# A graph layer and a mixture of experts in one kernel: scatters, bias adds, tile loads and block rows are put in another order

## Chip, cores and metric

The kernel runs on one NeuronCore of a Trainium2 chip. The metric is the device time in microseconds (us), and the time of a kernel is the median of its runs.

## What is computed

The input is a matrix x of 6250 nodes with 256 features, and a list of 206,250 edges that is sorted by destination. First comes an attention layer over the graph, then a mixture of 16 experts of which each node uses two. Cut to what matters:

```
xn  = layernorm(x);  hh = (xn @ W) as 8 heads of 32
e   = exp(leaky_relu(s_src[src] + s_dst[dst]))          # per edge and head
out = segment_sum(hh[src] * e / segment_sum(e), dst)     # per node
x   = x + elu(layernorm(out + xn) * gamma + beta)

y   = layernorm(x)
top-2 experts of y @ gate_w + gate_b, their softmax weights g
moe = sum over the two of g * (relu(y @ w1[e] + b1[e]) @ w2[e] + b2[e])
x   = x + layernorm(y + moe) * gamma2 + beta2
```

## The kernel before

**The edge loop.** The edges are cut into tiles of 128 and 31 tiles make a chunk (`CT`), so there are 52 chunks. A chunk is worked on in four groups of 8, 8, 8 and 7 tiles (`GROUPS`). For each tile, GpSimd (POOL) issues one indirect DMA that gathers 128 rows of the table, with 280 floats each, into a buffer `hx` (L199). A group has one `hx`, and there are four of them. VectorE builds two sets of one-hot matrices (`oh` L977, `ohT` L984), TensorE fetches the destination's part with them (`pm` L992), VectorE makes the edge weights and multiplies the gathered rows in place (L1008), and TensorE sums the rows into the accumulator `agg` (L1011). A group's `hx` is free again after its last `agg` matmul. At the end of a chunk the accumulator goes to `carry` (L1025) and is stored in `accd`. The destination values of a chunk (`abw`, `dlr`) are loaded two chunks ahead by `fetch`, at the start of a chunk, on the queue of SyncE (SP).

**Node blocks.** The nodes form 49 blocks of 128. Once all edges of a block are in, `node_block` loads its sums (`a`, L570) and rows (`xb`, L574) on SP, normalises, leaves y in `acc[:, b, :]` (L602) and finds the top two experts. It is called at the end of the chunk that completes the block.

**Parts and rounds.** The blocks are divided into rounds, and the rounds into parts (`ROUNDS`). When the last block of a part is done, `part_due` calls `routing`, which gives every pair of node and expert a row (`pos`), and puts three sorts of work into queues: `scat`, two scatters for each block, which write y to a buffer in DRAM by expert (`scatter`, L800, an indirect DMA of POOL); `bias`, one step for each block, which adds the two experts' second bias to `acc` (`biases`, L815 to L820); and `due`, the expert tiles that are full. A round's last part flushes all tiles that are left. There are 143 tiles in all.

**A tile** passes through four steps, one group apart: `weights` loads its rows (`xr`, L834) and w1; `turned` loads w2 and transposes the rows (L851); `hidden` multiplies by w1 (L860) and applies the ReLU (L869); `rows_out` multiplies by w2 (L875), copies to `yr` (L877) and stores it in `yg`. All its loads are on SP.

**`some`** is called after each group and takes from the queues: up to four scatters; one bias step if no scatter is waiting; then the next step of each tile under way; then one new tile, if its part has no scatter waiting. A bias add changes the rows that the scatters of its block read, so it must wait for them. The sum `pb` lies in PSUM in a tile `pt`, of which there is one for all transposes and small products.

**After the loop** the queues are emptied, and `result` gathers each node's two expert rows (`got`, L899), adds them, normalises and stores the block.

The order in which the instructions finally stand on each engine is set by a scheduler of the language, which keeps to the dependencies and may let an instruction pass others that are not ready.

Of the kernel before, what the change touches and what calls it, by code (L numbers as in the profile page):

```python
# [10 lines left out]
F32 = mybir.dt.float32  # L11
# [9 lines left out]
P = 128  # L21
# [4 lines left out]
LARGE = 40.0  # L26
CT = 31
GROUPS = (8, 8, 8, 7)
SLACK = 24


ROUNDS = ((10, 14, 18, 22, 26, 30, 34, 36), (43,), (49,))


@with_exitstack
def kernel(
# [20 lines left out]
    nc = tc.nc  # L57
    nc.scalar.preload_act_table_set("natural_log_exp_and_others")
    N, C = x.shape
# [8 lines left out]
    NK = -(-NE // CE)  # L68
# [11 lines left out]
    parts = []  # L80
# [101 lines left out]
    acc = const.tile([P, NB, C], F32, name="acc")  # L182
# [28 lines left out]
    with tc.tile_pool(name="a1", bufs=1) as a1, tc.tile_pool(name="a3", bufs=3) as a3, tc.tile_pool(  # L211
        name="aps", bufs=4, space=bass.MemoryType.PSUM
# [92 lines left out]
        for n in GROUPS:  # L305
# [11 lines left out]
        pb = aps.tile([P, 2 * H], F32, name="ph")  # L317
        nc.tensor.matmul(
            pb, lhsT=ex.to_broadcast([2 * H, P]), rhs=ident[: 2 * H, : 2 * H], start=True, stop=True
# [41 lines left out]
        when = {}  # L361
# [184 lines left out]
    with tc.tile_pool(name="w2", bufs=2) as w2_, tc.tile_pool(name="w3", bufs=3) as w3_, tc.tile_pool(  # L546
        name="rt", bufs=1
# [10 lines left out]
        def clear(r):  # L558

            for t in range(0, PAGES[r], ZR):  # L560
                n = min(ZR, PAGES[r] - t)
                nc.sync.dma_start(
                    xg[r][t * P : (t + n) * P, :].rearrange("(p j) c -> p j c", p=P),
                    zero[:, None, :].to_broadcast([P, n, C]),
                )
# [231 lines left out]
        def scatter(i, b, k):  # L797
            r = parts[i][2]
            n = P if b < NB - 1 else LAST
            t = nc.gpsimd.indirect_dma_start(  # L800
                out=xg[r][:, :],
                out_offset=bass.IndirectOffsetOnAxis(ap=pos[k][:n, b : b + 1], axis=0),
                in_=acc[:n, b, :],
                in_offset=None,
            )
            for _, o in scattered[r]:
                tc.declare_no_dep(t.ins, o.ins, reason="each pair has a row of its own")
            for o in read[r]:
                tc.declare_no_dep(t.ins, o.ins, reason="a tile that was due takes no more pairs")
            scattered[r].append((i, t))  # L810

        def biases(i, b):

            pt = wk.tile([E, P], F32, name="pt")
            nc.tensor.transpose(pt, shares[i][:, b - parts[i][0], :], ident)  # L815
            gt = e2.tile([E, P], F32, name="gt")
            nc.scalar.copy(gt, pt)
            pb = wk.tile([P, C], F32, name="pt")
            nc.tensor.matmul(pb, lhsT=gt, rhs=b2r, start=True, stop=True)
            nc.vector.tensor_add(acc[:, b, :], acc[:, b, :], pb)  # L820

        taken = []
        stored = []
# [92 lines left out]


        scat, due, bias = deque(), deque(), deque()
        at = [None, None, None]

        def some():
            for _ in range(min(4, len(scat))):
                scatter(*scat.popleft())
            if bias and not scat:
                biases(*bias.popleft())
            if at[2]:
                rows_out(*at[2])
            at[2] = hidden(*at[1]) if at[1] else None
            at[1] = turned(*at[0]) if at[0] else None
            at[0] = None  # L930
            if due and not any(t[0] == due[0][0] for t in scat):
                t = due.popleft()
                at[0] = weights(*t)

        def part_due(i):
            lo, hi, _, _, mt = parts[i]
            assert not any(t[0] < i - 1 for t in bias)
            routing(i)
            scat.extend((i, b, k) for b in range(lo, hi) for k in range(2))
            bias.extend((i, b) for b in range(lo, hi))  # L940
            due.extend((i, j) for j in range(mt))
# [4 lines left out]
        def fetch(k):  # L946

            after = fetched[-2][2:] if k > 1 else ()
            r0 = load(base_i[:, k : k + 1], 0, N - 1, engines=(ET.SP,), after=after)
            abw = w3_.tile([P, S3], BF16, name="abw", bufs=4)  # L950
            nc.sync.dma_start(abw, abd[ds(r0, P), :])
            dlr = w3_.tile([P, CT, P], U8, name="dlr")
            t0 = k * CT
            came = nc.sync.dma_start(
                dlr.rearrange("p t e -> p (t e)"),
                dlb[t0 : t0 + CT, :].rearrange("t e -> (t e)").partition_broadcast(P),
            )
            fetched.append((abw, dlr, came))

        weighed = []  # L960
        carry = None
        fetch(0)
        fetch(1)
        for k in range(NK):
            after = used[-2] if k > 1 else ()
            if k + 2 < NK:
                fetch(k + 2)
            abw, dlr, _ = fetched[k]
            t0 = k * CT
            agg = wps.tile([P, RA], F32, name="agg")  # L970
            g0 = 0
            for n in GROUPS:
                with ExitStack() as order:
                    if len(weighed) > 1:
                        order.enter_context(tc.issue_after(weighed[-2].ins))
                    oh = w3_.tile([P, n, P], F32, name="oh")
                    nc.vector.tensor_tensor(  # L977
                        oh,
                        along[:, None, :P].to_broadcast([P, n, P]),
                        dl[:, t0 + g0 : t0 + g0 + n, None].to_broadcast([P, n, P]),  # L980
                        ALU.is_equal,
                    )
                    ohT = w3_.tile([P, n, P], BF16, name="ohT")
                    nc.vector.tensor_tensor(  # L984
                        ohT,
                        dlr[:, g0 : g0 + n, :],
                        along[:, None, P:].to_broadcast([P, n, P]),
                        ALU.is_equal,
                    )
                pm = wps.tile([P, n * (S3 + H)], F32, name="pm")  # L990
                for g in range(n):
                    nc.tensor.matmul(  # L992
                        pm[:, g * S3 : (g + 1) * S3], lhsT=ohT[:, g, :], rhs=abw, start=True, stop=True
                    )
                hx, gathered = early.pop(0) if k == 0 else gather(k, g0, n)
                uv = w3_.tile([P, n, 2 * H], F32, name="uv")
                with ExitStack() as order:
                    if weighed:
                        order.enter_context(tc.issue_after(weighed[-1].ins))
                    nc.vector.tensor_reduce(  # L1000
                        uv, pm[:, : n * S3].rearrange("p (n t h) -> p n h t", n=n, t=3), AX.X, ALU.add
                    )
                nc.vector.tensor_tensor(uv, uv, hx[:, :, RA:], ALU.mult)  # L1003
                wt = pm[:, n * S3 :].rearrange("p (n h) -> p n h", n=n)
                nc.vector.tensor_tensor(wt, uv[:, :, :H], uv[:, :, H:], ALU.max)
                rows = hx[:, :, :RA].rearrange("p n (h d) -> p n h d", h=H)
                weighed.append(
                    nc.vector.tensor_tensor(rows, rows, wt.unsqueeze(3).to_broadcast([P, n, H, D1]), ALU.mult)  # L1008
                )
                for g in range(n):  # L1010
                    nc.tensor.matmul(  # L1011
                        agg,
                        lhsT=oh[:, g, :],
                        rhs=hx[:, g, :RA],
                        start=(g0 == 0 and g == 0),
                        stop=(carry is None and g0 + g == CT - 1),
                    )
                g0 += n
                some()
            if carry is not None:  # L1020
                shift = w2_.tile([P, P], F32, name="shift")
                nc.vector.tensor_scalar(shift, imp, down[:, k - 1 : k], None, op0=ALU.is_equal)
                nc.tensor.matmul(agg, lhsT=shift, rhs=carry, start=False, stop=True)
            carry = w2_.tile([P, RA], F32, name="carry")
            nc.scalar.copy(carry, agg)  # L1025
            r1 = load(base_w[:, k : k + 1], 0, DUMP, engines=(ET.Activation,), after=after)
            sent = nc.scalar.dma_start(accd[ds(r1, P), :], carry)
            used.append((sent,))
            for b in when.get(k, ()):
                node_block(b)  # L1030
                for i, p in enumerate(parts):
                    if b == p[1] - 1:
                        part_due(i)
            if k < len(ROUNDS):
                clear(k)
        while scat or due or bias or any(at):
            some()
        for i, p in enumerate(parts):
# [35 lines left out]
```

## Time and profile before

| | |
|---|---|
| median of 3 runs | 3372.06 us (3367.0 to 3377.96) |
| profiled execution | 2816.95 us, its span 2814.9 us |
| granted TensorE clock, mean | 0.817 |
| last gather of the loop / last tile stored | 2458 us / 2783 us after the span's start |
| busiest engines | TensorE 1842.8 us, POOL 1765.1 us, VectorE 1606.7 us |
| moved by DMA | 549 MB, 195 GB/s |

The profile shows one execution, and that execution was shorter than the timed runs. Durations below are from it. In the lines of the profile PE is TensorE, DVE is VectorE, ACT is ScalarE, POOL is GpSimd and SP is SyncE. A group's line gives its line in the code, the engine, the operation, what it writes and reads and how often, then its busy time and the mean in ns, then the engine's idle time ahead of it and what ended most of that. A line of waits gives the total in us, how often, and the longest. A line of the timeline gives the start, the duration, and in brackets the idle time before it and what ended it; "issue" means that nothing which the profile shows was waited for.

### The profile page before, as it was taken

What the parts mean: (1) busy time and instruction counts of PE and PEld (TensorE: products, weight loads), DVE (VectorE), ACT (ScalarE), POOL (GpSimd) and SP (SyncE); (2) the same over time, 40 slices, a digit from 0 to 9 for tenths busy, and PEclk for the clock granted to TensorE, in tenths of its full rate; (3) what the DMA queues carried; (4) which work ended last, traced back from release to release, by engine and by line L of the source; (5) the groups of instructions that cost most, each with busy time, mean ns of one, the idle gap of its engine ahead of it and who ended that gap; (6) DMA issues with size and microseconds to landing.
All of it is one profiled execution on the core that took longest, in us unless ns stands there. A gap on an engine that the chain in (4) does not pass through costs nothing. (4 is left out here: it accounts for less than half of the span.)

```text
span 2814.9 us, 33324 instructions
## 1 busy us (share of the span) xinstructions
PE 1842.8 (65%) x9507; PEld 1480.1 (53%) x9507; DVE 1606.7 (57%) x3479; ACT 447.1 (16%) x1606; POOL 1765.1 (63%) x1866
## 2 busy tenths in 40 slices
PE   7456666656656737638648638646888877866674
PEld 5334444435535526527536427535677666754564
DVE  7646666664763754845737645736456746645521
ACT  4100000001001102002011002010222212222332
POOL 3577777777774774766747765757476776617501
PEclk9777777867877968969869769868898989977898
DMA  7795554546547547547556547556788877848986
GB/s 211 206 318 149 139 143 133 144 137 214 141 135 208 168 133 237 148 142 225 143 167 211 140 139 228 143 163 191 236 266 260 261 229 241 265 137 289 298 277 188
DMA packets 374371, 549.11 MB, mean 195 GB/s; under 512 B 97974, under 2 KB 271500, under 8 KB 374180
## 3 DMA queue, kind: packets, MB, share of 16 engines
q0 software_dynamic: 89904, 263.85, 32.8%
q1 hardware_dynamic: 232408, 237.42, 27.4%
q10 hardware_dynamic: 51868, 45.63, 4.8%
q8 instruction: 78, 1.28, 0.2%
q14 instruction: 113, 0.93, 0.1%
HBM read 468.55 MB, written 78.15 MB: 194 GB/s over the span
## 5 line engine op out<-in xcount | busy, mean ns | idle before, releaser
L199 POOL DMA_INDIRECT hx<-table,src_sb x1612 | 1543.8, 958 | 714.4 <-issue 416.1
L1011 PE MATMUL agg<-hx,oh 128*128 128x264 f32 x3224 | 994.3, 469 | 336.0 <-DVE hx L1008 335.6
L1011 PEld LDWEIGHTS agg<-hx,oh 128*128 128x128 f32 x3224 | 733.4, 236 | 515.1 <-DVE hx L1008 363.8
L1008 DVE TENSOR_TENSOR hx<-hx,pm 128x2112 f32<-128x2112 f32 x208 | 474.3, 2280 | 2.4
L875 PE MATMUL po<-w2s,hT 128*128 128x256 f32 x1144 | 303.7, 404 | 58.8 <-ACT hT L869 56.3
L860 PEld LDWEIGHTS ph<-xt,w1s 128*128 128x128 f32 x2288 | 298.1, 204 | 32.9 <-issue 13.4
L860 PE MATMUL ph<-xt,w1s 128*128 128x128 f32 x2288 | 307.7, 289 | 9.2 <-DMA w1s<-in_L_ffn_w_dram 4.6
L977 DVE TENSOR_TENSOR oh<-along,dl 128x1024 f32<-128x1024 f32 x208 | 244.9, 1177 | 44.6 <-PE agg L1011 44.6
L875 PEld LDWEIGHTS po<-w2s,hT 128*128 128x128 f32 x1144 | 213.9, 199 | 102.0 <-ACT hT L869 73.5
L984 DVE TENSOR_TENSOR ohT<-dlr,along 128x1024 bf16<-128x1024 uint8 x208 | 245.0, 1178 | 3.2 <-DMA dlr<-dlb 3.2
L1003 DVE TENSOR_TENSOR uv<-uv,hx 128x128 f32<-128x128 f32 x208 | 59.3, 285 | 277.3 <-DMA hx<-table,src_sb 218.4
L869 ACT ACTIVATE hT<-ph,b1s 128x128 f32<-128x128 f32 x572 | 163.2, 367 | 278.4 <-PE ph L860 218.6
L899 POOL DMA_INDIRECT got<-yg,pos x98 | 97.3, 993 | 169.9 <-DMA yg<-yr 133.2
L820 DVE TENSOR_TENSOR acc<-acc,pt 128x256 f32<-128x256 f32 x49 | 20.6, 420 | 298.1 <-DMA xg<-acc,pos 191.8
L1000 DVE TENSOR_REDUCE uv<-pm 128x128 f32<-128x384 f32 x208 | 111.7, 537 | 100.7 <-PE pm L992 100.6
L992 PE MATMUL pm<-abw,ohT 128*128 128x48 bf16 x1612 | 75.6, 186 | 137.2 <-DVE ohT L984 111.8
L992 PEld LDWEIGHTS <-ohT 128*128 128x128 bf16 x1612 | 66.5, 98 | 176.6 <-DVE ohT L984 130.8
L191 ACT ACTIVATE mv<-mv,eps 128x1 f32<-128x1 f32 x98 | 28.9, 295 | 808.5 <-DVE mv L188 744.6
L800 POOL DMA_INDIRECT xg<-acc,pos x98 | 95.8, 978 | 90.2 <-DVE pf L728 60.6
L851 PE MATMUL pt<-ident,xr 128*128 128x128 f32 x286 | 60.2, 294 | 97.1 <-DMA xr<-xg 64.5
L815 PE MATMUL pt<-ident,gs 128*16 128x128 f32 x49 | 16.1, 328 | 162.0 <-DVE acc L820 156.6
L905 DVE SCALAR_TENSOR_TENSOR acc<-got,gate,acc 128x256 f32<-128x256 f32 (+1 forms) x98 | 45.4, 477 | 123.7 <-DMA got<-yg,pos 123.2
(233 smaller groups left out, 1354.8 us busy)
## 6 DMA issues: line engine op xcount, KB each, us to landing
w1s<-in_L_ffn_w_dram SPq DMA_DIRECT2D x143, 512.0 KB
w2s<-in_L_ffn_w_dram SPq DMA_DIRECT2D x143, 512.0 KB
hx<-table,src_sb POOLq DMA_INDIRECT x1612
dlr<-dlb SPq DMA_DIRECT2D x52, 496.0 KB
xr<-xg SPq DMA_DIRECT2D x143, 128.0 KB
yg<-yr ACTq DMA_DIRECT2D x143, 128.0 KB
xg<-zero SPq DMA_DIRECT2D x16, 1024.0 KB
accd<-carry ACTq DMA_DIRECT2D x52, 132.0 KB
```

The source lines that it names most:

```text
L199: t = nc.gpsimd.indirect_dma_start(out=hx[:, g, :], out_offset=None, in_=table[:, :], in_offset=bass.IndirectOffsetOnAxis(ap=src_sb[:, c : ...
L800: t = nc.gpsimd.indirect_dma_start(out=xg[r][:, :], out_offset=bass.IndirectOffsetOnAxis(ap=pos[k][:n, b : b + 1], axis=0), in_=acc[:n, b, :],
L860: nc.tensor.matmul(ph[:, f, :], lhsT=w1s[:, k, f * P : (f + 1) * P], rhs=xt[:, k, :], start=(k == 0), stop=(k == KC - 1),)
L869: nc.scalar.activation(hT[:, f, :], ph[:, f, :], AF.Relu, bias=b1s[:, f : f + 1])
L875: nc.tensor.matmul(po, lhsT=hT[:, f, :], rhs=w2s[:, f, :], start=(f == 0), stop=(f == FC - 1))
L899: nc.gpsimd.indirect_dma_start(out=got[:n], out_offset=None, in_=yg[parts[i][2]][:, :], in_offset=bass.IndirectOffsetOnAxis(ap=pos[k][:n, ...
L977: nc.vector.tensor_tensor(oh, along[:, None, :P].to_broadcast([P, n, P]), dl[:, t0 + g0 : t0 + g0 + n, None].to_broadcast([P, n, P]), ALU. ...
L984: nc.vector.tensor_tensor(ohT, dlr[:, g0 : g0 + n, :], along[:, None, P:].to_broadcast([P, n, P]), ALU.is_equal,)
L992: nc.tensor.matmul(pm[:, g * S3 : (g + 1) * S3], lhsT=ohT[:, g, :], rhs=abw, start=True, stop=True)
L1000: nc.vector.tensor_reduce(uv, pm[:, : n * S3].rearrange("p (n t h) -> p n h t", n=n, t=3), AX.X, ALU.add)
L1008: nc.vector.tensor_tensor(rows, rows, wt.unsqueeze(3).to_broadcast([P, n, H, D1]), ALU.mult)
L1011: nc.tensor.matmul(agg, lhsT=oh[:, g, :], rhs=hx[:, g, :RA], start=(g0 == 0 and g == 0), stop=(carry is None and g0 + g == CT - 1),)
```

## The change

- `ROUNDS`: the first round ends at block 33 instead of 36 and has seven parts instead of eight; the second ends at 42 instead of 43.
- `LAG`: the tiles and bias steps of a part may start three groups after the group that issued its last scatter. `some` counts the groups, and `come` compares.
- `biases` copies the bias from PSUM to a buffer in SBUF (of the name `yr`), and `biased` adds it to `acc` one group later.
- The blocks that a chunk completes are kept in `summed`, and `blocks` works on them after the first group of the next chunk. After the last chunk they follow at once.
- `fetch(k + 2)` is called after the second group of chunk k.

```diff
+LAG = 3
-ROUNDS = ((10, 14, 18, 22, 26, 30, 34, 36), (43,), (49,))
+ROUNDS = ((10, 14, 18, 22, 26, 30, 33), (42,), (49,))
...
             nc.tensor.matmul(pb, lhsT=gt, rhs=b2r, start=True, stop=True)
-            nc.vector.tensor_add(acc[:, b, :], acc[:, b, :], pb)
+            bs = e2.tile([P, C], F32, name="yr")
+            nc.scalar.copy(bs, pb)
+            return b, bs
+
+        def biased(b, bs):
+            nc.vector.tensor_add(acc[:, b, :], acc[:, b, :], bs)
...
-        at = [None, None, None]
+        at = [None] * 4
+        groups = [0]
+        stored_by = {}
+
+        def come(q):
+            return q and groups[0] >= stored_by.get(q[0][0], groups[0] + 1)
 
         def some():
+            groups[0] += 1
             for _ in range(min(4, len(scat))):
-                scatter(*scat.popleft())
-            if bias and not scat:
-                biases(*bias.popleft())
+                t = scat.popleft()
+                scatter(*t)
+                stored_by[t[0]] = groups[0] + LAG
+            if at[3]:
+                biased(*at[3])
+            at[3] = biases(*bias.popleft()) if come(bias) else None
             if at[2]:
                 rows_out(*at[2])
...
-            if due and not any(t[0] == due[0][0] for t in scat):
+            if come(due) and not any(t[0] == due[0][0] for t in scat):
                 t = due.popleft()
                 at[0] = weights(*t)
...
+        def blocks(bs):
+            for b in bs:
+                node_block(b)
+                for i, p in enumerate(parts):
+                    if b == p[1] - 1:
+                        part_due(i)
...
         for k in range(NK):
-            if k + 2 < NK:
-                fetch(k + 2)
...
                 some()
+                if g0 == GROUPS[0]:
+                    blocks(summed)
+                    summed = []
+                elif g0 == sum(GROUPS[:2]) and k + 2 < NK:
+                    fetch(k + 2)
...
-            for b in when.get(k, ()):
-                node_block(b)
-                for i, p in enumerate(parts):
-                    if b == p[1] - 1:
-                        part_due(i)
+            summed.extend(when.get(k, ()))
...
+        blocks(summed)
         while scat or due or bias or any(at):
             some()
```

## The prediction

> **What bounds the kernel now.** I read the busy shares first. No engine is full over the span, so the limit must be sought stage by stage. The groups then show gathers (L199) as the one large group whose idle time is mostly "issue".
>
> ```profile
> PE 1842.8 (65%) x9507; PEld 1480.1 (53%) x9507; DVE 1606.7 (57%) x3479; ACT 447.1 (16%) x1606; POOL 1765.1 (63%) x1866
> ...
> L199 POOL DMA_INDIRECT hx<-table,src_sb x1612 | 1543.8, 958 | 714.4 <-issue 416.1
> ```
>
> A gather is 0.95 us and the next starts 0.30 us later: 1.25 us each, 31 a chunk, 39 us. Chunks 2 to 11 ran their gathers in 39.3 us each with no pause. So POOL's queue sets the pace of the loop, and the time to win there is POOL's pauses. The waits of POOL alone, from the end of the first chunk's gathers to the last gather (132 to 2460 us):
>
> ```profile
> POOL hx L199 <- issue: 407.3, 1337, 0.3
> POOL hx L199 <- PE agg L1011: 189.2, 78, 24.5
> POOL hx L199 <- PE pt L608: 36.7, 12, 4.6
> POOL hx L199 <- PE pm L992: 27.4, 16, 14.9
> ```
>
> The first line is the 0.30 us. The pauses over 1.5 us sum to 227 us: six of about 24 us (24.3, 23.7, 24.0, 24.5, 24.1, 24.1: 144.7), six of 2.4 to 4.4 us in the chunk after a part's scatters (22.5), 38.3 between 1990 and 2130 us (14.9, 2.6, 6.8, 6.8, 7.2), 8.0 at the start and 14 of single ones near the end. Each 24 us pause stands directly behind a part's eight scatters. The timeline of POOL and that of VectorE at one of them:
>
> ```profile
> 1057.50 0.96 POOL L800 DMA_INDIRECT xg<-acc,pos  x1 [0.30 <-issue]
> 1058.77 0.96 POOL L800 DMA_INDIRECT xg<-acc,pos  x1 [0.30 <-issue]
> 1083.40 0.98 POOL L199 DMA_INDIRECT hx<-table,src_sb  x1 [23.68 <-PE agg L1011]
> ```
>
> ```profile
> 1029.12 0.53 DVE L602 TENSOR_SCALAR acc<-xb,mv 128x256 f32<-128x256 f32 x1
> 1053.66 0.42 DVE L820 TENSOR_TENSOR acc<-acc,pt 128x256 f32<-128x256 f32 x1 [24.01 <-DMA xg<-acc,pos]
> ```
>
> VectorE reaches the bias add at 1029.65 and waits 24.0 us for scatters that stand on POOL's queue behind 16 more gathers. Meanwhile POOL fills all four hx buffers, scatters, and must then wait until VectorE and TensorE have freed one. TensorE has four tiles to do, in part or whole, ahead of that agg: it is busy 20.2 of the 24 us from 1060. So **the add's wait costs nothing by itself; the pause of POOL that follows costs 24 us.**
>
> **What the Trainium skill says.** "PSUM — Partial Sum Buffer", Engine vs sequencer instructions: the ScalarE, VectorE and GpSimd queues are strict FIFO and matmuls keep program order. The trace agrees: VectorE ran nothing in the 24.01 us. "Perfetto Trace Analysis", DMA Instruction — SWDGE: a GpSimd DMA's slice ends with its descriptors, not with the data. It agrees: the second scatter's slice ends at 1052.13, the add that needs it starts at 1053.66. "TensorE: Matmul & The Clock Gate", Part 1: an idle TensorE is throttled. It agrees: clock 0.50 from 1049 to 1060 us, then 0.79 in the catch-up.
>
> **The change part by part.** A scheduler decides the queues, so I counted in both built programs how many gathers stand ahead of a part's scatters on POOL, and how many weighted groups (L1008) stand ahead of its first bias add on VectorE, both in chunks.
>
> - *LAG, and the add a group later.* Before, six parts have scatters at 18.52, 22.52, 26.52, 30.52, 35.52, 39.52 and adds at 17.50, 21.50, ...: 1.02 apart, just the four hx buffers, so nothing is left to gather after the scatters. After: 18.52 against 17.75, 35.52 against 34.75 (0.77); 22.06, 26.06, 30.06 against 21.50, 25.50, 29.50 (0.56); 38.3 against 38.5. The add still waits in five parts, but POOL has runway: 8 gathers (10 us) where the distance is 0.77, 14 (17.5 us) where it is 0.56. And tiles come one a group instead of five in half a chunk: ahead of the agg that POOL needs stands one, not four. A tile is 16 ph and 8 po matmuls, 1.95 + 1.9 us plus transposes, 4.3 us in all; three fewer bring the agg from 23.7 to about 11 us after the last scatter. Left: 11 less 10 is 1, I take 3, in two parts; 0 in three, I take 2; 0 in the sixth: 12 of 144.7. Bounds: 0, and 12 a part (72). The 22.5 that follow the catch-ups I halve to 11 (bounds 0 and 22.5). The trace has one neighbour of such a distance: the first part, 13.26 against 12.75, with 20 scatters. POOL paused only 3.5 us there.
> - *New: scatters stand closer to their routing.* At 22.06 POOL may arrive before pos is written. Unseen in the loop; from 0 to 5 us in four parts, I take 10 in all.
> - *ROUNDS.* Nine parts instead of ten; the late part with four scatters at 41.26 goes. The 38.3 us stand there, with an 18.5 us wait of VectorE for a block row (den L577) that SP issued late. The flush stays at a tile a group, so I keep 20 (bounds 8 and 40). Two scatters leave the loop: -2.5. One routing fewer, some 60 small VectorE instructions of 0.2 us, beside other work: 0. The tile count is 143 in both (81 + 33 + 29 for 87 + 29 + 27), but 45 instead of 42 tiles are unfinished at the end of the loop. From 2733 to 2783 us a tile takes 4.56 us, TensorE-bound; from 2536 to 2740, with DMA at 0.91, about 7.1. Three cost 13.7, at most 21. The last part has seven blocks instead of six: the six results after the last tile took 28.5 us, so +4.7. Its 14 scatters: +2.5. **Tail +20.9.**
> - *Block rows into the next chunk.* 49 blocks, each with two loads on SP (a, xb), a store on ACT's queue, 17 VectorE, 6 ScalarE and 4 TensorE instructions. SP's wait for the stored carry was 364 us in total, and tile loads stand behind it. Asked a group later, the store (5.5 us) is mostly down. The add of the first group covers it. VectorE's order keeps den where it was, so I book 0 here; bounds -15 and +10.
> - *Destination loads after the second group.* 50 pairs of DMAs on SP, 496 KB the larger. They still come a chunk and a half (58 us) before use and no longer hold SP for the free buffer (429 us waited at L954). VectorE's wait for dlr was 3.2 us in all. Cost 0; if tile loads ahead of them held SP more than 58 us, chunks would stall, up to 10 in the flush.
> - *Bias through SBUF.* 49 ScalarE copies of 0.37 us, 18 us on an engine at 16%: 0. PSUM tile pt is freed by the copy, so TensorE's 156.6 us behind the add (PE pt L815) go; that is part of the catch-up above, not counted again. The yr buffers are now shared with rows_out, two copies a group; 0 to 5, taken 0.
>
> **Sum.** Pauses after: 12 + 11 + 20 + 8 + 14 = 65 of 227, so -162, +10, -2.5, hence about -154; I round to -150. With the tail -130: 2817 becomes 2687, a factor of 0.954. The median of the runs shown is 3372, 1.197 times the profiled execution, and the trace doesn't show where the 555 us lie. Stretched evenly it gives 3216, as a plain difference 3242. I take **3225**.
>
> **Rivals.** *The flush is bound by TensorE (0.15 within the faster cases).* TensorE is busy 504 of 640 us from 1850 to 2490. Spreading wins nothing after chunk 37, all 38 stay and perhaps 20 more come: 2725, about 3265. *The wait only moves (0.10).* For it: five adds still stand ahead of their scatters, and the tile's xr load still waits on SP for all eight. Against: the first part's 3.5 us. With 12 us left a part and the flush unchanged the loop wins 65, the tail takes 28: 2780, about 3330. *Slower (0.09).* One mechanism: agg still comes 24 us after the scatters plus the runway, because xr lands late and TensorE keeps its order, so POOL pauses as before, and only the tail's three tiles, block and scatters remain: at 7.1 us a tile +28, so 2845, about 3405. It decides once pauses of more than about 205 us are left, which is 20 a part plus all others. *The change does not do what it says:* for block rows and destination loads nearly so, since the scheduler leaves VectorE's order there; booked at 0 above.
>
> **How the numbers follow.** Main case 0.62 (3145 to 3260; the low end with nothing left of the six pauses and a flush at 8: -190 times 1.197). TensorE-bound flush 0.15, moved wait 0.10, no change 0.04, slower 0.09. A measurement of this kernel tells some 0.3% from no change, 10 us. Faster 0.87, same 0.04, slower 0.09. The range reaches from 3130 to 3340 and leaves out the last two cases and a little at the low end.
>
> **What would show it.** Right: POOL's pauses behind eight scatters fall from 24 to under 6 us, its waits for agg L1011 from 189 to under 70, the last gather at about 2310 instead of 2458, and from there to the end some 20 us more than 356. Each step wrong: pauses of 20 us again (runway), a wait of POOL's scatters for pf in the loop (routing), den waits over 15 us (block rows), VectorE or TensorE waiting for dlr (fetch). The whole is wrong if the last gather comes after 2440.

## The result, and the profile after

The changed kernel took 3335.99 us (median of 4 runs, 3314.25 to 3339.61), the kernel before 3375.01 beside it (4 runs): ratio 0.987, with an interval of 0.982 to 0.992. That is 1.3% faster, where 4.4% were forecast. It lies in the range, but the forecast gain was more than three times the measured one. (The ratios here and below leave out runs that lie over 1.5% above the fastest of their kernel, so they are not exactly the quotients of the medians.)

The page of the changed kernel, its busy shares and its gathers:

```profile
PE 1893.8 (57%) x9497; PEld 1523.3 (46%) x9497; DVE 1609.9 (48%) x3415; ACT 464.6 (14%) x1652; POOL 1757.3 (53%) x1866
...
L200 POOL DMA_INDIRECT hx<-table,src_sb x1612 | 1534.9, 952 | 1185.6 <-issue 434.0
```

A gather takes 0.95 us, as before. But the gathers now have 1185.6 us of idle time ahead of them; in the execution that the prediction was read from they had 714.4. The waits of POOL in the same execution:

```profile
POOL hx L200 <- issue: 434.0, 1422, 0.8
POOL hx L200 <- PE agg L1033: 267.8, 40, 18.9
...
POOL hx L200 <- remote: 97.0, 37, 4.8
POOL hx L200 <- PE pt L857: 91.3, 10, 19.9
```

The wait for `agg` was to fall from 189 us to under 70; it is 268. ("remote" is a release that the trace can't place.) The last gather comes at 2925 us, where 2310 was forecast.

The reason is neither in the diff nor in noise. **The kernel before runs at two speeds, by chip.** On three chips it takes 2810 to 2834 us, on the others 3303 to 3410, and no series of runs showed both. (Each chip was measured in one series only, so that a chip keeps its speed is not shown.) The profiled execution that the prediction was read from, 2817 us, is like the runs of the first kind of chip, called A here. The runs that it was compared with, median 3372, are like those of the second, called B. The same changed kernel, on a chip of kind A:

```profile
PE 1809.3 (69%) x9497; PEld 1461.7 (56%) x9497; DVE 1607.3 (61%) x3415; ACT 462.8 (18%) x1652; POOL 1769.0 (68%) x1866
...
L200 POOL DMA_INDIRECT hx<-table,src_sb x1612 | 1545.4, 959 | 524.9 <-issue 418.9
```

```profile
POOL hx L200 <- issue: 418.9, 1374, 0.3
...
POOL hx L200 <- PE agg L1033: 38.5, 62, 7.1
```

Of the gathers' 524.9 us of idle time 418.9 are the gaps of 0.30 us between two of them. There the change took the kernel from 2819.3 to 2623.5 us: ratio 0.930, interval 0.927 to 0.933. POOL's wait for `agg` falls as the prediction said, and the gain is larger than its factor of 0.954.

### The profile page after: what moved, and what is told of

Read it like the earlier page. It is cut to its first block, busy times and chain, and to the rows that moved or that the text cites. A ratio compares the mean times of both kernels' runs of the same rounds, so it can differ in the third digit from the quotient of the medians.

```text
span 3331.8 us, 33273 instructions
## 1 busy us (share of the span) xinstructions
PE 1893.8 (57%) x9497; PEld 1523.3 (46%) x9497; DVE 1609.9 (48%) x3415; ACT 464.6 (14%) x1652; POOL 1757.3 (53%) x1866
## 3 DMA queue, kind: packets, MB, share of 16 engines
q8 instruction: 78, 1.28, 0.1%
## 5 line engine op out<-in xcount | busy, mean ns | idle before, releaser
L200 POOL DMA_INDIRECT hx<-table,src_sb x1612 | 1534.9, 952 | 1185.6 <-issue 434.0
L1033 PE MATMUL agg<-hx,oh 128*128 128x264 f32 x3224 | 971.7, 463 | 339.1 <-DVE hx L1030 199.3
L881 PE MATMUL po<-w2s,hT 128*128 128x256 f32 x1144 | 346.1, 445 | 321.6 <-ACT hT L875 198.7
L881 PEld LDWEIGHTS po<-w2s,hT 128*128 128x128 f32 x1144 | 233.7, 218 | 377.6 <-ACT hT L875 214.8
L866 PEld LDWEIGHTS ph<-xt,w1s 128*128 128x128 f32 x2288 | 314.2, 212 | 45.1 <-issue 18.0
L866 PE MATMUL ph<-xt,w1s 128*128 128x128 f32 x2288 | 322.7, 297 | 19.2 <-ACT xt L859 10.7
L614 PE MATMUL pt<-gw,yt 128*128 128x16 f32 x196 | 40.8, 325 | 137.3 <-ACT yt L611 76.4
L614 PEld LDWEIGHTS pt<-gw,yt 128*128 128x128 f32 x196 | 38.3, 269 | 150.1 <-ACT yt L611 83.6
L1049 DVE TENSOR_SCALAR shift<-imp,down 128x128 f32<-128x128 f32 x51 | 15.5, 304 | 172.0 <-remote 88.1
L616 DVE TENSOR_TENSOR lg<-pt,gtb 128x16 f32<-128x16 f32 x49 | 8.5, 174 | 175.9 <-PE pt L614 97.5
```

Of the source, the lines that this page charges most:

```text
L200: t = nc.gpsimd.indirect_dma_start(out=hx[:, g, :], out_offset=None, in_=table[:, :], in_offset=bass.IndirectOffsetOnAxis(ap=src_sb[:, c : ...
L866: nc.tensor.matmul(ph[:, f, :], lhsT=w1s[:, k, f * P : (f + 1) * P], rhs=xt[:, k, :], start=(k == 0), stop=(k == KC - 1),)
L881: nc.tensor.matmul(po, lhsT=hT[:, f, :], rhs=w2s[:, f, :], start=(f == 0), stop=(f == FC - 1))
L1033: nc.tensor.matmul(agg, lhsT=oh[:, g, :], rhs=hx[:, g, :RA], start=(g0 == 0 and g == 0), stop=(carry is None and g0 + g == CT - 1),)
```

## The experiments

All ratios are to the kernel before on the same chip, with their 95% intervals.

| run | kind of chip | us | ratio |
|---|---|---|---|
| the change | B | 3336.0 | 0.987 (0.982 to 0.992) |
| e1, before once more | B | 3351.8 | 1.002 (0.999 to 1.005) |
| e2, ROUNDS only | B | 3293.7 | 0.984 (0.979 to 0.989) |
| e3, LAG only | B | 3302.4 | 0.987 (0.980 to 0.994) |
| e4, moves only | B | 3344.8 | 1.004 (1.000 to 1.007) |
| f1, ROUNDS and LAG | A | 2696.2 | 0.957 (0.955 to 0.959) |
| f2, no bias | A | 2748.4 | 0.975 (0.973 to 0.977) |
| f5, half of the aggregation matmuls | A | 2700.8 | 0.959 (0.957 to 0.962) |
| f6, half of their width | A | 2702.2 | 0.959 (0.957 to 0.961) |
| g1, the change | A | 2623.5 | 0.930 (0.927 to 0.933) |
| g2, ROUNDS and LAG | A | 2698.3 | 0.958 (0.955 to 0.960) |
| g3, as f6 | A | 2706.8 | 0.959 (0.956 to 0.963) |
| g4, as f5 | A | 2708.4 | 0.960 (0.956 to 0.964) |
| h1, half of the gathers | B | 2575.3 | 0.770 (0.767 to 0.773) |
| h2, the change with half of the width | B | 3193.1 | 0.957 (0.953 to 0.962) |
| h3, the change without the fetch move | B | 3316.6 | 0.992 (0.989 to 0.995) |
| i1, the change without the fetch move | A | 2623.7 | 0.931 (0.929 to 0.934) |
| i2, ROUNDS and LAG | A | 2701.3 | 0.958 (0.955 to 0.961) |
| i3, LAG only | A | 2732.2 | 0.969 (0.965 to 0.972) |

From the starts of the gathers, the time of a chunk in us (one execution each; chunks 2 to 11 have no tiles, chunks 22 to 29 hold two parts with their scatters and tiles), and the sum in us of all pauses of POOL over 1.5 us ahead of a gather from chunk 13 on. Two executions on kind B can differ by 2 us a chunk with the same work: e1 and e2 have the same parts up to chunk 29.

| kernel | kind | chunks 2 to 11 | chunks 22 to 29 | pauses |
|---|---|---|---|---|
| before (read for the prediction) | A | 39.3 | 48.4 | 219 |
| LAG only (i3) | A | 39.3 | 45.3 | 117 |
| ROUNDS and LAG (i2) | A | 39.3 | 45.2 | 106 |
| the change (g1) | A | 39.4 | 41.6 | 23 |
| before (e1) | B | 47.0 | 57.1 | 661 |
| ROUNDS only (e2) | B | 47.3 | 59.3 | 628 |
| LAG only (e3) | B | 47.1 | 54.9 | 593 |
| the change | B | 47.6 | 56.8 | 622 |
| the change with half of the width (h2) | B | 47.0 | 53.6 | 495 |
| half of the gathers (h1) | B | 30.8 | 43.2 | |

### First series: the parts one by one (kind B)

**e1**, the kernel before, unchanged.

> The kernel before, unchanged, to get a profile of an execution as long as the timed ones; the one that the prediction used was 2817 us, the timed runs are 3375. Theory A (runway): outside the parts' scatters POOL's gathers run back to back at 39 us a chunk here too, the 555 us lie elsewhere, and POOL pauses about 24 us behind each part's scatters. Theory B (another pace): POOL pauses in nearly every chunk, chunks 2 to 11 take 45 to 50 us each instead of 39.3, and POOL's waits for hx buffers sum to over 600 us, of which the six pauses behind scatters are a minor share. Ratio to the kernel before 1.00 in both.

Theory B held: 47.0 us a plain chunk. The waits of POOL:

```profile
POOL hx L199 <- issue: 440.9, 1426, 2.1
POOL hx L199 <- PE agg L1011: 365.1, 48, 26.5
...
POOL hx L199 <- PE pm L992: 124.4, 18, 14.7
POOL hx L199 <- remote: 115.0, 46, 4.8
```

The pauses of 24 to 27 us behind six parts' scatters are there, but from chunk 13 on some 510 us of others as well. They stand in nearly every chunk, also where no tile is under way. Where it doesn't pause, a gather takes the same 1.25 us; POOL's queue does not set the pace here.

**e2, e3, e4**, one part of the change each:

```diff
-ROUNDS = ((10, 14, 18, 22, 26, 30, 34, 36), (43,), (49,))
+ROUNDS = ((10, 14, 18, 22, 26, 30, 33), (42,), (49,))          # e2: this alone
```

```diff
-            if due and not any(t[0] == due[0][0] for t in scat):
+            if come(due) and not any(t[0] == due[0][0] for t in scat):   # e3: LAG, come, biased;
                                                                 # old ROUNDS, old places
```

```diff
-            for b in when.get(k, ()):                            # e4: blocks in the next chunk and
-                node_block(b)                                    # fetch after the second group;
+            summed.extend(when.get(k, ()))                       # no LAG, old ROUNDS
```

> The kernel before with the new ROUNDS alone: nine parts, 143 tiles, the late part with four scatters gone, 40 tiles instead of 41 left at the end of the loop by the built order, seven blocks instead of six in the last part. Theory A: the 38 us of pauses between 1990 and 2130 us fall to some 20, the last part costs 5: 0.99 to 1.00. Theory B: pauses of that size are all over the loop and one part fewer is worth little: 0.995 to 1.005.

> The kernel before with the LAG of three groups and the bias copied to SBUF and added a group later, with the old ROUNDS and block rows and destination loads where they were. By the built order the adds stand at 17.75, 21.75 ... against scatters at 18.52, 22.52 ... (0.77 chunks apart instead of 1.02), and 44 tiles instead of 41 are left at the end. Theory A: a runway of 8 gathers, 10 us, at each of six parts and three tiles fewer ahead of the agg: -60 to -130 us in the loop, +14 in the tail: 0.965 to 0.985. Theory B: the pauses behind the scatters shrink but the pace is set elsewhere: 0.985 to 1.005.

> The kernel before with block rows taken up after the first group of the next chunk and destination loads after the second group, all else as before. Theory A (booked at 0 in the prediction): 0.995 to 1.005. Theory B: the block rows' chain (carry stored, a loaded, some 17 VectorE steps, transposes) is part of what sets the pace of every chunk, so moving it changes all 52: 0.97 to 0.99, or slower by as much if it comes to stand ahead of a group.

Measured: 0.984, 0.987, 1.004. e2 gained more than either theory had, e3 fits theory B, and e4 fits theory A: the block rows don't set the pace. Multiplied the three would be 0.974; all together are 0.987, so on kind B the parts don't add up. With LAG the pauses behind the scatters fell from 24 to between 7 and 13 us in six parts, yet the chunks between them (mean of two), 44 to 48 us before, took 48 to 51. Part of what the pauses lost came back there.

### Second series: what paces a chunk (kind A)

**f1**, the change without its moves; **f2**, the kernel before without bias adds; **f5** and **f6**, the kernel before with less work for TensorE:

```diff
-                if g0 == GROUPS[0]:                              # f1, against the changed kernel
-                    blocks(summed)
-                    summed = []
-                elif g0 == sum(GROUPS[:2]) and k + 2 < NK:
-                    fetch(k + 2)
+            blocks(when.get(k, ()))                              # at the chunk's end, as before;
+                                                                 # fetch at its start
```

```diff
-                biases(*bias.popleft())                          # f2
+                bias.popleft()
```

```diff
-                for g in range(n):                               # f5
+                for g in range(0, n, 2):
                     nc.tensor.matmul(agg, lhsT=oh[:, g, :], rhs=hx[:, g, :RA], ...)
```

```diff
+                    wide = RA if g0 + g == 0 else RA // 2        # f6
-                    nc.tensor.matmul(agg, lhsT=oh[:, g, :], rhs=hx[:, g, :RA], ...)
+                    nc.tensor.matmul(agg[:, :wide], lhsT=oh[:, g, :], rhs=hx[:, g, :wide], ...)
```

> The changed kernel without its moves: new ROUNDS and LAG, block rows and destination loads at their old places. Theory C (the moves cost 33 us once tiles are spread: pairs of chunks 20-22 to 30-32 took 50.5 + 64.4 us a chunk with the moves and 50.9 + 60.7 with LAG alone): ratio to the kernel before 0.974 to 0.982, a pair of chunks with scatters at 60 to 61 us a chunk again. Theory D (ROUNDS and LAG don't add up because both spread the same tiles over the flush, the moves are innocent): 0.985 to 0.989, as the whole change.

> The kernel before with its bias adds left out (no gate transposes, no bias matmuls, no adds; the shares of b2 are missing from the result), so VectorE never waits for a part's scatters. Theory of the prediction (the wait of the add makes POOL pause 24 us a part, and the pauses are what there is to win): all six pauses go, ratio 0.95 to 0.96. Theory B (the eight tiles of a part cost TensorE and its handoffs 4.4 to 5.2 us each wherever they stand; the pause is only where this shows): the gain is that of the left-out bias work and a few us a part, ratio 0.98 to 0.99, and a pair of chunks with scatters plus the next pair still takes over 215 us (227 before).

> The kernel before with every second aggregation matmul (L1011) left out: 16 of a chunk's 31 are left, half of the edges are missing from the sums. Theory A (POOL's queue sets the pace of plain chunks): chunks 2 to 12 stay at 47 us each, ratio over 0.99. Theory B (TensorE with its handoffs sets it): plain chunks fall to 39.3 to 41 us, where POOL's gathers become the bound, ratio 0.86 to 0.92.

> The kernel before with the aggregation matmuls half as wide (132 of 264 columns, all but each chunk's first; half of the heads' sums are missing), as many instructions and semaphore updates as before. Theory A (POOL's queue): no change, over 0.99. Theory B1 (the time of the array's columns is what TensorE is short of): as much as with half of the matmuls, 0.86 to 0.92. Theory B2 (the number of matmuls and of their semaphore updates: in ordinary executions TensorE's updates come 1.4 us apart where the records of the matmul pairs stand 0.44 us apart): less than a third of that gain, 0.96 to 0.99.

This series ran where the kernel before took 2817.3 us, so the expectations, made for kind B, have to be read with that. f1 gave 0.957, about what the prediction had forecast for the whole (0.954). In f5 and f6 the plain chunks stayed at 39.1 us with half of the aggregation's matmuls or half of their width: on kind A TensorE's work does not set the pace there, as it would not if POOL's queue does. The six pauses of 24 us became 10.8 to 15.4 us. But less work for TensorE is not the only difference: in both kernels' built order the scatters also stand eight gathers earlier (chunk 18.26 instead of 18.52), and the pause comes behind these eight gathers. The runs don't part the two.

f2 shows how much the add's wait is worth. POOL's waits in it:

```profile
POOL hx L199 <- PE pt L851: 82.1, 12, 10.4
POOL hx L199 <- PE agg L1011: 74.1, 68, 10.1
```

With no add at all the six pauses were still 9.2 to 10.4 us long, and pauses of 5.7 and some 3.5 us follow each of them. Chunks 22 and 23 together took 106.1 us instead of 115.3; over the six parts such a pair gained 6 to 9 us. So the add's wait, with the bias work itself, is the smaller part of the pauses. The rest remains without it, and 82 us of POOL's waits are put down to the transposes of the part's tiles (`pt`, L851). The measured 0.975 lies between the two theories.

### Third series: the whole change on kind A

**g1** is the changed kernel, **g2** is f1 again, **g3** and **g4** are f6 and f5 again.

> The changed kernel once more, beside the kernel before on the same chip. The kernel before takes about 2815 us on one chip (its profiled execution ahead of the prediction, and the runs beside the kernel without its moves) and about 3350 on others. Theory E (the change is worth what the pauses of POOL are worth, and these only count on a chip where POOL's gathers set the pace): ratio 0.955 to 0.975 where before takes 2815 us, 0.983 to 0.992 where it takes 3350. Theory F (the whole change is worth 1% anywhere, because its moves take back what LAG gives): 0.98 to 0.99 on either.

> The changed kernel without its moves, again. Where before takes 2815 us it gave 0.957. Where before takes 3350 us, theory E: 0.98 to 0.99, as the whole change; the moves are worth nothing to either side. Theory F: 0.960 to 0.975, clearly under the whole change.

> The kernel before with aggregation matmuls of 132 columns instead of 264 (half of the heads' sums are missing). Where before takes 2815 us it gave 0.959, plain chunks unchanged at 39.1 us. Where before takes 3350 us (plain chunks 47 us): theory B1 (columns of TensorE's array are the pace there): plain chunks at 39 to 41 us, 0.86 to 0.90. Theory B2 (matmuls and their semaphore updates are, whatever their width): plain chunks stay at 45 to 47, 0.95 to 0.98.

> The kernel before with 16 instead of 31 aggregation matmuls a chunk (half of the edges are missing from the sums). Where before takes 2815 us it gave 0.959, plain chunks 39.1. Where before takes 3350 us: theories B1 and B2 both have plain chunks at 39 to 42 us and 0.86 to 0.92; if they stay at 47 us, neither holds, and the pace is set by something other than TensorE.

Theory E named the right cause, but the gain was larger than it had it: 0.930 for 0.955 to 0.975. Theory F fell. g2, g3 and g4 repeated 0.958, 0.959 and 0.960. The waits of POOL in i2, the same kernel as f1 and g2 (without the moves):

```profile
POOL hx L200 <- PE pt L816: 45.2, 5, 9.4
POOL hx L200 <- PE pt L609: 39.8, 14, 6.6
POOL hx L200 <- PE agg L1035: 38.2, 61, 10.3
```

and POOL behind the last scatter of a part, first in i2, then in g1:

```profile
1041.96 0.96 POOL L801 DMA_INDIRECT xg<-acc,pos  x1 [0.30 <-issue]
1051.92 0.98 POOL L200 DMA_INDIRECT hx<-table,src_sb  x1 [9.00 <-PE pt L816]
```

```profile
1017.40 0.96 POOL L801 DMA_INDIRECT xg<-acc,pos  x1 [0.31 <-issue]
1018.67 0.98 POOL L200 DMA_INDIRECT hx<-table,src_sb  x1 [0.30 <-DVE ohT L1006]
```

The 9 us, and some 4 us a part later where POOL's wait is put down to `pt` of a block row (L609), are gone with the moves. In g1 the two chunks with a part's scatters, 22 and 23 as well as 26 and 27, take 88.6 and 88.0 us. POOL's queue alone needs about that for 62 gathers and 8 scatters: 2 x 39.1 + 8 x 1.26 = 88.3. The loop is at POOL's floor there.

### Fourth series: what slows kind B

The trace holds the times of each semaphore update. On kind B they tell what the matmul records don't. Here is TensorE in e1, in a plain chunk, then VectorE, then TensorE's next step:

```profile
333.99 0.54 PE L992 MATMUL pm<-abw,ohT 128*128 128x48 bf16 x15
351.29 0.69 PE L608 MATMUL pt<-ident,acc 128*128 128x128 f32 x2 [16.76 <-DVE acc L602]
```

```profile
334.41 0.17 DVE L188 BATCH_NORM_AGGREGATE mv<-s 128x2 f32<-128x6 f32 x1
349.77 0.51 DVE L1000 TENSOR_REDUCE uv<-pm 128x112 f32<-128x336 f32 x1 [15.19 <-remote]
```

By the records `pm` is done at 334.5 us. VectorE, which waits for TensorE's semaphore, reads it at 349.77, and a load of SP that waits for the same semaphore goes out at 349.77 too. And POOL in that time:

```profile
333.82 0.95 POOL L199 DMA_INDIRECT hx<-table,src_sb  x1 [0.30 <-PE agg L1011]
...
352.56 0.95 POOL L199 DMA_INDIRECT hx<-table,src_sb  x1 [0.30 <-issue]
364.92 0.94 POOL L199 DMA_INDIRECT hx<-table,src_sb  x1 [11.40 <-DVE hx L1008]
```

POOL gathers without a break until all four buffers are full, at 353.5. Then it stands still for 11.4 us, and in that time TensorE catches up. The same over the whole loop: each interval between two successive updates of TensorE (between 180 and 2900 us), with the mean share of the gathers' DMA queue at that moment.

| interval | A, before: number, gather share | B, e1: number, gather share |
|---|---|---|
| 0.42 to 0.47 us (a matmul pair at full clock) | 1338, 0.34 | 392, 0.12 |
| 0.84 to 0.92 us (at half clock) | 360, 0.39 | 165, 0.14 |
| 1.28 to 1.50 us | 26, 0.36 | 162, 0.38 |

The gathers' mean share is 0.32 and 0.30. On kind A the interval has nothing to do with gathers. On kind B TensorE hands over at its usual pace mostly where few gathers run, and at a third of it where they run. It isn't the clock: the granted clock is 0.50 or 1.00 in every record, at which a pair takes 0.88 and 0.44 us. The traces of kind B lack some updates (e1 has 2501 of 2921), and some 30 of the 162 may be three steps of 0.44 us with two updates lost.

A comparison that lost updates don't touch is plainer. In the loop, from 180 us on, each of the 2489 updates of the execution on kind A comes within 0.05 us of the recorded end of an instruction of TensorE. Of e1's 2114, 589 come more than 1 us after the last such end, while only 1.3% of VectorE's updates and 0.2% of ScalarE's are so late. The delays cover 811 us of e1's loop; the gathers' mean share is 0.37 in them and 0.27 outside. Late ones can come in bursts, eight within 0.34 us at 323.2 us, where a single pair takes 0.44 us or more; which points to the update being held back there and not the matmul. The Trainium skill, "Perfetto Trace Analysis", Tensor Engine Instruction, says that TensorE's recorded end is computed and not observed, and that the semaphore goes out only when PSUM has acknowledged the write. This case agrees on kind B, where the update can come 15 us after the recorded end (334.5 us above); on kind A the two coincide. Whether the acknowledgement is what is late no run shows.

That is a coincidence in time so far. The next runs took away one side each: **h1** gathers only 16 of 31 batches of rows and uses each for two batches of edges (its sums are those of other rows, and VectorE multiplies in two halves), with as many instructions of TensorE (9507), though fewer of them update a semaphore (1720 instead of 2921); **h2** halves the width of the aggregation in the changed kernel, the same edit as f6; **h3** is the change without the fetch move.

```diff
-        for g in range(n):                                       # h1
+        for g in range(0, n, 2 if k else 1):
...
-                        rhs=hx[:, g, :RA],
+                        rhs=hx[:, g // 2 if k else g, :RA],
```

```diff
-                elif g0 == sum(GROUPS[:2]) and k + 2 < NK:       # h3, against the changed kernel
-                    fetch(k + 2)
...
+            if k + 2 < NK:                                       # at the chunk's start, as before
+                fetch(k + 2)
```

> The kernel before with 16 instead of 31 gathers in each chunk after the first: each gathered batch of rows is used for two batches of edges (the sums are those of wrong rows; VectorE's elementwise work is done in two halves, TensorE's instructions are the same in number and shape). Where before takes 2815 us: POOL's 39 us a chunk fall to 20, and VectorE and TensorE set the pace, 28 to 33 us a plain chunk. Where before takes 3350 us (47 us a plain chunk): theory G (gathers in flight slow TensorE's handoffs): a plain chunk falls to 26 to 35 us, and the updates of TensorE are 1.4 us apart less often; theory B (TensorE is slow there by itself): 43 to 47 us.

> The changed kernel with aggregation matmuls of 132 columns instead of 264 (half of the heads' sums are missing). Where before takes 2815 us: POOL's pauses are gone already, so only the rest of 23 us and a little of the catch-ups is left to win: 0.915 to 0.93. Where before takes 3350 us: theory B1 (columns): plain chunks at 39 to 41 us, 0.84 to 0.90. Theory B2 or G (matmuls and their updates, whatever their width, while gathers run): plain chunks stay at 45 to 47 us, 0.94 to 0.98.

> The changed kernel with its destination loads at their old place, ahead of the chunk: block rows moved, fetch not. Where before takes 2815 us: if the block rows give the 75 us of the moves, 0.930 to 0.935; if the destination loads do, 0.955 to 0.958. Chunks after a part's scatters show which: 39.2 us (the whole change) or 42 to 43 with pauses of 4 us at pt L609 (without moves). Where before takes 3350 us: 0.98 to 0.99 either way.

h1: plain chunks fell from 47.0 to 30.8 us, the time from 3346.7 to 2575.3. From its page and its waits of POOL:

```profile
PE 1793.3 (70%) x9507; PEld 1461.5 (57%) x9507; DVE 1660.8 (65%) x3887; ACT 450.8 (18%) x1606; POOL 1029.9 (40%) x1101
```

```profile
POOL hx L199 <- PE agg L1016: 649.6, 96, 24.5
```

As many matmuls as before, more VectorE instructions, and yet a third less a chunk. POOL, at 40% of the span, is now far from being the bound: it waits 650 us for TensorE's `agg`. With theory B (TensorE slow there by itself) 43 to 47 us would have stayed. Of TensorE's updates in the loop 78 of 1145 are over 1 us late, 7% instead of 28. h2: plain chunks stayed at 47.0 us with half of the columns, so there TensorE's array time is not what kind B is short of. Theory G, the gathers in flight hold up TensorE's hand-offs, fits both runs. One rival is left: h1 took away updates as well as gathers, and theory B2 (each update costs, whatever the gathers do) fits both runs too. Against it stands that TensorE keeps its usual pace where few gathers run (392 steps of some 0.44 us at a share of 0.12); f5, which has fewer updates (2208) and all gathers, ran on kind A only. As to the moves, e4's 1.004 shows no gain from them on kind B, and h3's 0.992 beside the change's 0.987 tells nothing of them.

How the gathers do it is open. "Trainium Architecture — The Big Picture", What this means for kernel authors, has it that engine accesses and DMA can't contend in SBUF; no run here locates the place. Nor is it known what distinguishes the chips. Since the traces of kind B also lack updates that those of kind A have, the recording itself may have a part in it; no run here excludes that. ROUNDS and LAG without the moves have no run on kind B.

### Fifth series: which move (kind A)

**i1** is h3's kernel, **i2** is f1's, **i3** is e3's.

> The changed kernel with its destination loads at their old place: block rows moved, fetch not. Where before takes 2815 us: 0.930 to 0.937 if the block rows give the 75 us of the moves, 0.953 to 0.958 if the destination loads do, between them if both are needed. I take the block rows: without moves POOL paused at pt L609, which is a step of the block rows, and with them it doesn't. Where before takes 3350 us: about 0.99, as the first time.

> The changed kernel without its moves. Where before takes 2815 us: 0.957 again. Where before takes 3350 us: since gathers slow TensorE there, the tiles cost about the same wherever they stand, so 0.980 to 0.992, as LAG alone (0.987) and the whole (0.987); if the moves take something back, 0.965 to 0.978.

> The kernel before with LAG and the later add alone, old ROUNDS, old places. Where before takes 2815 us: pauses behind six parts' scatters fall from 24 to 9 us, so about 6 x 15 = 90 us less in the loop and 10 to 15 more in the tail (44 tiles for 41): 0.970 to 0.978, the rest to 0.957 being that of ROUNDS. Where before takes 3350 us: 0.987 again.

Measured 0.931, 0.958, 0.969. Here the parts do stack: LAG 3.1%, ROUNDS another 1.1, the block rows another 2.7, the destination loads nothing (2623.7 us without their move, 2623.5 with it, on two chips). i3's six pauses of 8.9 to 9.3 us were as expected, its ratio a little below the range; its tail was 16 us longer than the kernel's before (372 against 356).

## Why the prediction was right and wrong

**The step that failed** is the last of its sum: "Stretched evenly it gives 3216". It took an execution of 2817 us for a short sample of the runs of 3372, with the same limits, only slower. The runs of 3372 have another limit. "POOL's queue sets the pace of the loop" was read off chunks of 39.3 us; on kind B they take 47, with POOL pausing in nearly each, where TensorE's hand-offs come late (589 of 2114 in e1). The forecast of 130 us became 147 by the stretching; measured were 39 (3375 to 3336). POOL's pauses there went from 661 to 622 us only (e1 against the change, one execution each, which can differ by as much with the same work). That 3336 lies in the range is luck: its upper end was kept for a rival (the wait only moves, about 3330) that isn't what happened. The working itself noted that the trace doesn't show where the 555 us lie. Since nearly a sixth of the time was unaccounted for, the range should have reached to no change with more than the 0.04 it gave.

On the kind of chip that the working was read from, its steps stand as follows.

- **The six pauses of 24 us.** Forecast 12 us left of 144.7: 3 in two parts, 2 in three, 0 in the sixth. Measured in g1: 6.5 and 5.3 in the two where scatters and first bias add stand 0.77 chunks apart, 0.3 (no pause) in the three of 0.56, and the sixth none: 11.8. That the sum was right is luck, as two parts were taken too low and three too high. The size at 0.77 was wrong: 11 less 10 us of runway was to leave 1. In g1 the pauses come behind eight gathers, so the runway was there and `agg` came later than forecast; in f1, where all five stand 0.77 apart, 8.9 to 9.2 us come directly behind the scatters, with no runway at all.
- **The pauses that follow.** 11 forecast of 22.5; none over 1.5 us left.
- **Scatters too close to their routing.** 10 forecast; in g1 the only such wait is the last part's, after the loop, 44.4 us, which was 60.6 before. Nothing in the loop.
- **The late part and the flush.** 20 forecast of 38.3; 11.2 measured (2.1, 7.1 and 2.0, in chunks 39 and 40). The rival that TensorE bounds the flush fell on kind A: chunks 41 to 46 take 38.9 to 39.9 us.
- **Other pauses.** 8.0 at the start stayed (7.9); the 14 of single ones went, which the working had kept. In all 31 us of 227 are left, where 65 were forecast.
- **The tail.** +20.9 forecast; -6.1 measured, 350.3 us from the last gather to the end instead of 356.4. Last tile to end took 33.8 instead of 31.5, +2.3 for the +4.7 of the seventh block and the +2.5 of scatters. The tiles were mis-sized: 46 instead of 45 were stored after the last gather, not three more, and they came 7.4 us apart until the last ten instead of 8.1.
- **Block rows, booked at 0** with bounds of -15 and +10. Worth 2.7% of 2817, 75 us. "VectorE's order keeps den where it was" looked at the wrong queue. What moved (seen by the runs without the moves, f1 and i2) was the part's scatters, from chunk 22.52 to 22.06 and the like in three parts, with the first bias add going from 21.75 to 21.50 only (0.56 chunks apart for 0.77), which gave POOL its runway, and the transposes of the block rows (L609), which no longer stand in TensorE's queue where POOL waits. POOL's pauses went from 106 us (i2) to 23 (g1). The distances of 0.56 were in the working, but under LAG, without the block rows that made them. The rival "the change does not do what it says" was wrong on the block rows and right on the destination loads.
- **Destination loads, booked at 0.** Right: i1 against g1.

So on kind A spans went from 2814.9 to 2618.5, -196 us where -130 were forecast, and the last gather to 2268 where 2310 were. "The whole is wrong if the last gather comes after 2440" decided rightly on kind B: 2925.

## What to carry to other kernels

Compare the profiled execution's time with the timed runs first. If they are a fifth apart, the profile may be of another regime, with other waits setting the pace, and then a sum of pauses can't be carried over by a factor. Where a step is moved, count anew how far apart every queue's partners stand, not only the queue that the step is written for.

## What the runs showed of the hardware

The same program took 2817 to 2819 us (medians) on three chips and 3347 and 3350 on two others, with the same durations of single instructions (a gather 0.95 us, 1.25 with its gap; a tile 4.5 us at the end of the tail on both). On the slower ones over a quarter of TensorE's semaphore updates in the loop (589 of 2114 in e1) came more than 1 us after the recorded end of its work, and steps of 1.28 to 1.50 us between updates fell where gathers by GpSimd ran; on the quicker ones all 2489 were punctual, with pairs 0.44 or 0.88 us apart. Half as many gathers took a plain chunk on a slower chip from 47.0 to 30.8 us; half as many columns of the aggregation's matmuls left it at 47.0. What fewer gathers would be worth on the quicker chips, and what larger ones would on either, was not tried.
